# Fetching ten of 391 groups of x1 rows with one-row DMAs issued by SP and ACT, in the second layer of a graph network

## The chip, the cores and the metric

The kernel runs on one core of one Trainium2 chip. The metric is the time of one execution on the device in microseconds (us); smaller is better. The engines go by their names in the profile: PE (TensorE, matrix products; PEld is its weight load), DVE (VectorE), ACT (ScalarE), POOL (GpSimd), SP (SyncE). ACT, POOL and SP also issue DMAs. Each engine works through its own list of instructions in order, and waits on semaphores that other engines or DMAs raise.

## What is computed

Two layers of message passing over a graph of 12,500 nodes with 48 features each and 200,000 edges, sorted by their target node `dst`. Cut to what matters:

```python
# layer 0
tmp = concatenate([x[dst], x[src], edge_attr_32], axis=1)
msg = relu(tmp @ W1 + b1) @ W2 + b2
x   = layernorm(x + segment_sum(msg, dst))          # called x1 in the kernel
# layer 1
m   = relu(x[src] + edge_attr_48)
x   = layernorm(x + (1 + eps) * x + segment_sum(m, dst))
```

The change is about `x[src]` of layer 1: for every edge the row of x1 (48 floats, 192 bytes) of its source node, which can be any node.

## The kernel before

**Groups and steps.** The edges are cut into 391 groups (`NCHUNK`) of 512: 128 partitions times 4 tiles (`TPC`). Partition p of group g holds four edges, and their source numbers stand in `src_i[p, 4g : 4g+4]`, which is in SBUF for the whole kernel. Each layer is a loop over steps k (`run`): in each step several stages work, each on a group of its own, some groups ahead of or behind k. The order of instructions on every engine is this program order; no scheduler moves them. What the engines wait for is decided by semaphores, so an engine may be many steps ahead of another as long as its data and buffers allow it.

**Layer 1** has, in this order in each step k:

- `fetch1(k+5)`: POOL issues four indirect DMAs (`gather`, L201), one for each tile; each fetches 128 rows of x1 from DRAM into the tile `xs`. There are ten `xs` buffers, and a buffer comes free when the DVE addition `m` of the group that used it is done.
- `fill1(k+2)`: DVE makes the one-hot matrix `hot` (L302). Every fifth group SP loads a chunk of five groups of edge features, `e48c` (L293, 480 KB, three buffers).
- `sum1(k-1)`: PE multiplies `hot` with the messages of group k-1 (L323, tile `pa`), DVE adds the result to the running sums `agg` (L318). If the group is the last of a segment (one of 14 blocks of 896 nodes), `finish1` follows: transposes, the layer norm on DVE with two ACT instructions within (L350, L354), and an SP store of the result (L386).
- `message1(k)`: DVE adds x1 rows and edge features, `m` (L495), then ACT applies relu, `msg` (L497).
- `lead1(k)`: one piece of `products()`, and now and then an SP load of a segment of x1 (`x_seg`).

**The groups that PE fetches.** 28 groups (26, 39, 52, ...; `PE_GROUPS`) are not gathered by POOL. `products()` makes their rows on PE: DVE turns source numbers into selection matrices `o` (L525), PE multiplies them with x1, which lies in SBUF in three bf16 pieces (L530), and adds up over all 98 blocks of 128 nodes. Two groups are made at a time. One step does four blocks: 4 DVE comparisons and 32 matmuls; 364 of the steps hold such a piece. The rows made this way are read by `m` as the tile `made`.

**Where x1 comes from.** Layer 0 ends each segment with `finish0`, whose result SP writes to `x1_dram` (L368). Since a source may be any node, every fetch of layer 1 waits for all 14 writes.

**In layer 0** POOL gathers the rows of x (tile `cat`), and SP does in each step a load of one number from SBUF into a register (L409, `off`) and a DMA whose address in DRAM is that register (L412, `wcat<-a`, 48 rows of 512 bytes), beside a chunk of edge features each fifth group (`e32c`, L293).

**ACT** does one relu a step in layer 1 and next to nothing else; **SP** issues a chunk load each fifth step, and 28 loads and stores of segments.

Of the kernel before, what the change touches and what calls it, by code (L numbers as in the profile page):

```python
# [24 lines left out]
F32 = mybir.dt.float32  # L25
# [6 lines left out]
P = 128  # L32
# [3 lines left out]
D = 48  # L36
# [5 lines left out]
NPAD = NT * Q  # L42
TPC = 4
CHUNK = P * TPC
NCHUNK = -(-E // CHUNK)
# [12 lines left out]
EC = 5  # L58
# [4 lines left out]
PIECES = 3  # L63
BPS = 4

PE_GROUPS = [FIRST + EVERY * i for i in range(NPE)]
assert PE_GROUPS[-1] < NCHUNK and NPE % BATCH == 0

assert NSEG * NB == NT
# [28 lines left out]
@with_exitstack  # L98
def gnn_kernel(
    ctx: ExitStack,  # L100
    tc: tile.TileContext,
    x: bass.AP,
    src: bass.AP,
    dst: bass.AP,
    e32: bass.AP,
    e48: bass.AP,
    w1: bass.AP,
    b1: bass.AP,
    w2: bass.AP,
    b2: bass.AP,  # L110
    eps: bass.AP,
    out: bass.AP,
):
    nc = tc.nc
    flag_pool = ctx.enter_context(tc.tile_pool(name="flag", bufs=1))
    dram = ctx.enter_context(tc.tile_pool(name="dram", bufs=1, space=bass.MemoryType.DRAM))
    flag = flag_pool.tile([1, 1], I32, name="flag")
    with ExitStack() as fast:
        windowed(fast, tc, dram, flag, x, src, dst, e32, e48, w1, b1, w2, b2, eps, out)
    misfit = nc.values_load(  # L120
        flag, engines=[mybir.EngineType.PE, mybir.EngineType.DVE, mybir.EngineType.Activation,
                       mybir.EngineType.Pool, mybir.EngineType.SP],
        min_val=0, max_val=2 * P,
    )
    with tc.If(misfit > 0), ExitStack() as slow:
        general(slow, tc, dram, x, src, dst, e32, e48, w1, b1, w2, b2, eps, out)


def windowed(ctx, tc, dram, flag, x, src, dst, e32, e48, w1, b1, w2, b2, eps, out):
    nc = tc.nc  # L130
# [3 lines left out]
    echunk = ctx.enter_context(tc.tile_pool(name="echunk", bufs=3))  # L134
    work = ctx.enter_context(tc.tile_pool(name="work", bufs=2))
    aggs = ctx.enter_context(tc.tile_pool(name="aggs", bufs=3))
    node = ctx.enter_context(tc.tile_pool(name="node", bufs=2))
# [4 lines left out]
    src_i = const.tile([P, NCHUNK * TPC], I32, name="src_i")  # L142
# [6 lines left out]
    def load_seg(table, s):  # L149
        x_seg[s] = seg.tile([Q, NB, D], F32, name="x_seg")  # L150
        nc.sync.dma_start(
            x_seg[s], table[s * SN : (s + 1) * SN, :].rearrange("(t p) d -> p t d", p=Q)
        )
# [43 lines left out]
    x1_dram = dram.tile([NPAD, D], F32, name="x1_dram")  # L197
    xp = const.tile([Q, NT, PIECES, D], BF16, name="xp")

    def gather(t, table, g, j):  # L200
        nc.gpsimd.indirect_dma_start(  # L201
            out=t, out_offset=None, in_=table,
            in_offset=bass.IndirectOffsetOnAxis(
                ap=src_i[:, g * TPC + j : g * TPC + j + 1], axis=0
            ),
        )
# [41 lines left out]
    def split_src():  # L248
# [3 lines left out]
        )[:, :, 0:TPC]  # L252
        last = src_i[:, PE_GROUPS[-1] * TPC : (PE_GROUPS[-1] + 1) * TPC]
        bits = node.tile([P, NPE, TPC], I32, name="bits")
# [31 lines left out]
    chunk = {}  # L286

    def load_edges(name, table, width, g):
        c = g // EC
        if g % EC == 0:  # L290
            n = min(EC, NCHUNK - g)
            chunk[name] = echunk.tile([P, EC, TPC * width], F32, name=name)
            nc.sync.dma_start(  # L293
                chunk[name][:, :n, :],
                table[g * CHUNK : (g + n) * CHUNK, :].rearrange(
                    "(c p t) d -> p c (t d)", p=P, t=TPC
                ),
            )
        return chunk[name][:, g % EC, :].rearrange("p (t d) -> p t d", t=TPC)

    def one_hot(o, g):
        nc.vector.tensor_tensor(  # L302
# [85 lines left out]
    def last_group(s):  # L388

        return max(g for g in range(NCHUNK) if low(g) < (s + 1) * SN)  # L390
# [6 lines left out]
    cat, ph, h, pm, hot = {}, {}, {}, {}, {}  # L397
# [6 lines left out]
    def fill0(g):  # L404
        e = load_edges("e32c", e32, DE, g)
        nc.scalar.activation(cat[g][:, :, W + D :], e, AF.Copy)
        one_hot(cat[g][:, :, :W], g)
        s = seg_of(g)
        at = nc.sync.value_load(  # L409
            off[0:1, g : g + 1], min_val=low(g) - seg_start(s), max_val=high(g) - seg_start(s)  # L410
        )
        nc.sync.dma_start(wcats[g % NW][0:W, :], a_dram[s][bass.ds(at, W), :])  # L412
# [65 lines left out]
    made = {}  # L478

    def fetch1(g):  # L480
        if g in PE_GROUPS:
            return
        cat[g] = cats.tile([P, TPC, D], F32, name="xs")
        for j in range(TPC):
            gather(cat[g][:, j, :], x1_dram, g, j)

    def fill1(g):
        hot[g] = work.tile([P, TPC, W], F32, name="hot", bufs=4)
        one_hot(hot[g], g)
        h[g] = load_edges("e48c", e48, D, g)  # L490

    def message1(g):
        m = work.tile([P, TPC, D], F32, name="m")
        xs = made.pop(g) if g in PE_GROUPS else cat.pop(g)
        nc.vector.tensor_tensor(m, xs, h[g], op=ALU.add)  # L495
        msg = work.tile([P, TPC, D], F32, name="msg1")
        nc.scalar.activation(msg, m, AF.Relu)  # L497
        h[g] = msg
# [10 lines left out]
    def place(first):  # L509

        which = psum.tile([Q, tiles, P], BF16, name="pt", bufs=2)
        for i in range(BATCH):
            which_e = work.tile([P, TPC, Q], BF16, name="which_e")
            for j in range(TPC):
                nc.vector.tensor_scalar(
                    which_e[:, j, :], iota_q, part[:, first + i, j : j + 1],
                    block[:, first + i, j : j + 1], op0=ALU.is_equal, op1=ALU.mult,
                )
            for j in range(TPC):
                nc.tensor.transpose(which[:, i * TPC + j, :], which_e[:, j, :], ident16)  # L520
        return which

    def select(which, b):
        o = onehots.tile([Q, tiles, P], BF16, name="o")
        nc.vector.tensor_scalar(o, which, float(b + 1), None, op0=ALU.is_equal)  # L525
        return o

    def multiply(ps, o, b):
        for k in range(tiles):
            nc.tensor.matmul(  # L530
                ps[k // PER][:, k % PER, :], o[:, k, :], xp[:, b, :, :],
                start=False, stop=False, skip_group_check=True,
            )

    def edge_of(ps, start):
        for t in ps:
            n = t.shape[1] * PIECES * D
            nc.tensor.matmul(
                t.rearrange("p k c d -> p (k c d)"), zeros[:, :P], zeros[:, :n],
                start=start, stop=not start,  # L540
            )
# [4 lines left out]
    def products():  # L546

        for first in range(0, NPE, BATCH):
            due = PE_GROUPS[first]
            which = place(first)  # L550
            ps = [
                psum.tile([P, min(PER, tiles - k * PER), PIECES, D], F32, name=name,
                          bufs=2 if name == "pt" else 1)
                for k, name in enumerate(SUMS)
            ]
            edge_of(ps, True)
            last = []
            for b in range(0, NT, BPS):
                now = [(b + i, select(which, b + i)) for i in range(min(BPS, NT - b))]
                for c, o in last:  # L560
                    multiply(ps, o, c)
                last = now
                yield due
            for c, o in last:
                multiply(ps, o, c)
            edge_of(ps, False)
            xs = work.tile([P, tiles, D], F32, name="made")
            for k, t in enumerate(ps):
                n = t.shape[1]
                nc.vector.tensor_reduce(  # L570
                    xs[:, k * PER : k * PER + n, :], t.rearrange("p k c d -> p k d c"),
                    AX.X, ALU.add,
                )
            for i in range(BATCH):
                made[PE_GROUPS[first + i]] = xs[:, i * TPC : (i + 1) * TPC, :]
            yield due

    work1 = products()

    def lead1(k):  # L580
        next(work1, None)
        for s in range(NSEG):
            if k == last_group(s) - 6:
                load_seg(x1_dram, s)

    run([(fetch1, -AHEAD), (fill1, -2), (sum1, 1), (message1, 0)], finish1, lead1)


# [209 lines left out]
```

## Time and profile before

| | |
|---|---|
| Time, median of 11 runs | 4841.38 us (4819.24 to 4860.51) |
| The profiled execution: its time / its span | 4848.64 us / 4846.9 us |
| Layer 1 in it: first and last start of `m` | 2549.7 us, 4833.8 us |
| First 320 starts of `m` / the other 71 | 1924.10 us / 360.20 us |
| Indirect DMAs of POOL in layer 1 | 1452, of 966 ns each |
| POOL idle before them until `m` freed a buffer | 463.2 us, in 152 places |
| ACT idle before its relu, until `m` was done | 1615.2 us, in 306 places |
| Mean granted clock of TensorE | 0.726 of full speed |

The profile is of one execution on the chip. Times are in us from the first instruction unless marked ns. "Busy" counts the engine's own work; register, branch and semaphore instructions and the issuing of DMAs are not counted, but the trace has their records, under an engine's name with a q (SPq, ACTq). In a list of waits a line gives the engine and the line of the code, what ended the wait, the total idle time in us, how often, and the longest one. "issue" is idle time in which an engine waited for nothing that the profile shows; "remote" is a releaser that it can't name. A row of the timeline gives start, duration, engine, line, operation, tiles (out<-in), shape, how many were merged, and in brackets the idle time before it and what ended it.

### The profile page before, as it was taken

The page shows a single profiled execution, that of the slowest core. Times are in us where ns is not written, and L with a number is a line of the kernel's source. Part 1 is how long each engine was busy: PE and PEld are TensorE (multiplying, and loading weights), DVE is VectorE, ACT ScalarE, POOL GpSimd, SP SyncE. Part 2 cuts the span into 40 slices and gives each one's busy share as a digit, 9 for nine tenths or more (in the row PEclk, how much of TensorE's full clock was granted, in tenths as well). Part 3 has the DMA queues.
Part 4 walks back from the last instruction along what each step waited for, and adds up shares of the span by engine and source line. Part 5 has one row for each costly group of instructions (what it writes and reads, how often), then busy time and mean ns, then how long its engine had stood idle before and what let it go on. Part 6 is the DMA issues. An engine that isn't in the chain of part 4 may idle for free. (4 is left out here: it accounts for less than half of the span.)

```text
span 4846.9 us, 67581 instructions
## 1 busy us (share of the span) xinstructions
PE 3171.6 (65%) x23396; PEld 2395.9 (49%) x23396; DVE 1899.0 (39%) x4618; ACT 563.2 (12%) x1329; POOL 2887.0 (60%) x3025
## 2 busy tenths in 40 slices
PE   4676676676776667767656666666666676666652
PEld 3454454454454445545435555555555555555541
DVE  1222222222222222222225555555555555555542
ACT  1111111111111111111110000000000000000000
POOL 5655655655665566566646565656565665655564
PEclk7777767777677777677767777777777777777765
DMA  2111111111111111111111111111111111111111
GB/s 53 32 38 38 33 36 36 35 35 38 35 37 38 31 36 39 38 32 38 33 32 30 33 30 39 34 35 34 35 34 36 34 40 34 30 39 35 34 31 35
DMA packets 293005, 171.68 MB, mean 35 GB/s; under 512 B 109664, under 2 KB 292400, under 8 KB 292656
## 3 DMA queue, kind: packets, MB, share of 16 engines
q0 software_dynamic: 96512, 74.31, 10.2%
q1 hardware_dynamic: 179248, 84.31, 6.4%
q10 hardware_dynamic: 16896, 8.69, 0.6%
q8 instruction: 185, 3.03, 0.3%
q14 instruction: 164, 1.34, 0.1%
HBM read 154.45 MB, written 12.62 MB: 34 GB/s over the span
## 5 line engine op out<-in xcount | busy, mean ns | idle before, releaser
L201 POOL DMA_INDIRECT cat<-in_x_dram,src_i x1564 | 1483.1, 948 | 971.1 <-issue 857.0
L201 POOL DMA_INDIRECT xs<-x_dram,src_i x1452 | 1401.9, 966 | 960.5 <-DVE m L495 463.2
L530 PEld LDWEIGHTS <-o 128*128 128x128 bf16 x10976 | 930.1, 117 | 591.5 <-issue 553.8
L525 DVE TENSOR_SCALAR o<-pt 128x1024 bf16<-128x1024 bf16 x1372 | 849.8, 679 | 56.3 <-remote 51.6
L424 PE MATMUL ph<-cat_t,wcat 128*128 128x512 f32 x782 | 621.9, 888 | 199.7 <-DVE cat_t L419 190.3
L530 PE MATMUL ph<-xp,o 128*128 128x144 bf16 x4116 | 636.1, 267 | 169.8 <-issue 162.1
L530 PE MATMUL pm<-xp,o 128*128 128x144 bf16 x4116 | 624.5, 267 | 151.8 <-issue 151.1
L318 DVE TENSOR_TENSOR agg<-agg,pa 48x48 f32 x782 | 153.3, 196 | 1306.1 <-remote 857.6
L419 DVE COPY cat_t<-pt 128x512 f32<-128x512 f32 x391 | 269.9, 690 | 874.7 <-PE pt L417 374.9
L432 PE MATMUL pm<-w_sb,h 128*128 128x48 f32 x3128 | 553.4, 332 | 79.1 <-ACT h L426 41.8
L530 PE MATMUL pt<-xp,o 128*128 128x144 bf16 x2744 | 501.8, 267 | 130.3 <-issue 129.6
L432 PEld LDWEIGHTS pm<-w_sb,h 128*128 128x128 f32 x3128 | 499.5, 243 | 113.5 <-ACT h L426 49.0
L323 PE MATMUL pa<-hot,msg 128*48 128x48 f32 x3128 | 317.3, 247 | 330.3 <-issue 206.8
L323 PE MATMUL pa<-cat,msg 128*48 128x48 f32 x3128 | 281.7, 249 | 376.8 <-issue 209.4
L426 ACT ACTIVATE h<-ph,b_sb 128x512 f32<-128x512 f32 x391 | 268.6, 687 | 1830.3 <-PE ph L424 779.6
L323 PEld LDWEIGHTS pa<-cat,msg 128*48 128x48 f32 x3128 | 226.8, 158 | 485.2 <-issue 300.4
L323 PEld LDWEIGHTS pa<-hot,msg 128*48 128x48 f32 x3128 | 239.0, 154 | 429.0 <-issue 264.1
L417 PEld LDWEIGHTS pt<-ident,cat 128*128 128x128 f32 x1564 | 278.0, 190 | 333.3 <-issue 317.2
L497 ACT ACTIVATE msg<-m 128x192 f32<-128x192 f32 x391 | 141.8, 363 | 2077.4 <-DVE m L495 1615.2
L434 DVE TENSOR_TENSOR msg<-pm,b_sb 128x192 f32<-128x192 f32 x391 | 137.9, 353 | 544.9 <-remote 218.2
L417 PE MATMUL pt<-ident,cat 128*128 128x128 f32 x1564 | 332.1, 353 | 1.9 <-issue 1.9
L424 PEld LDWEIGHTS ph<-cat_t,wcat 128*128 128x128 f32 x782 | 160.3, 254 | 215.6 <-DVE cat_t L419 205.3
(79 smaller groups left out, 1061.6 us busy)
## 6 DMA issues: line engine op xcount, KB each, us to landing
e48c<-in_e_dram SPq DMA_DIRECT2D x78, 480.0 KB
cat<-in_x_dram,src_i POOLq DMA_INDIRECT x1564
e32c<-in_e_dram SPq DMA_DIRECT2D x78, 320.0 KB
xs<-x_dram,src_i POOLq DMA_INDIRECT x1452
wcat<-a SPq DMA_DIRECT2D x391, 24.0 KB
a<-a ACTq DMA_DIRECT2D x14, 256.0 KB
a<-a ACTq DMA_DIRECT2D x14, 192.0 KB
x_seg<-in_x_dram SPq DMA_DIRECT2D x14, 168.0 KB
```

Of the source, the lines that this page charges most:

```text
L201: nc.gpsimd.indirect_dma_start(out=t, out_offset=None, in_=table, in_offset=bass.IndirectOffsetOnAxis(ap=src_i[:, g * TPC + j : g * TPC + ...
L318: nc.vector.tensor_tensor(cols, cols, pa, op=ALU.add)
L323: nc.tensor.matmul(pa, msg[:, j, :], hot[:, j, :], start=j == 0, stop=j == TPC - 1)
L417: nc.tensor.transpose(pt[:, j, :], cat[g][:, j, :], ident[:P, :P])
L419: nc.vector.tensor_copy(cat_t, pt)
L424: nc.tensor.matmul(ph, wcats[g % NW], h[g], start=True, stop=True)
L426: nc.scalar.activation(t, ph, AF.Relu, bias=b1_sb)
L432: nc.tensor.matmul(pm[:, j, :], h[g][:, j, :], w2_sb, start=True, stop=True)
L434: nc.vector.tensor_tensor(msg, pm, b2_sb[:, None, :].to_broadcast([P, TPC, D]), op=ALU.add)
L497: nc.scalar.activation(msg, m, AF.Relu)
L525: nc.vector.tensor_scalar(o, which, float(b + 1), None, op0=ALU.is_equal)
L530: nc.tensor.matmul(ps[k // PER][:, k % PER, :], o[:, k, :], xp[:, b, :, :], start=False, stop=False, skip_group_check=True,)
```

## The change

Ten groups are taken from POOL and fetched row by row: five by SP (67, 132, 197, 262, 327) and five by ACT (74, 139, 204, 269, 334). For each partition the engine loads that partition's four source numbers from `src_i` into registers (one load instruction), then issues four DMAs, each of one row of 192 bytes, whose address in `x1_dram` comes from a register. Each engine does two partitions, so eight DMAs, in each step; a group takes 64 steps and a 65th without a fetch. The first begins in step -5, the last ends in step 318. The rows are read by `m` as the tiles `rows_sync` and `rows_scalar`, two buffers each. Besides, `load_edges`, which both layers use, now issues the load of a chunk of edge features when the chunk before it is first used, five groups sooner; the first two chunks are loaded together.

```diff
+BY_ROW = {"sync": (67, 65, 2), "scalar": (74, 65, 2)}
+ROW_GROUPS = {
+    name: list(range(first, NCHUNK, every)) for name, (first, every, _) in BY_ROW.items()
+}
+ALL_ROW_GROUPS = sum(ROW_GROUPS.values(), [])
...
     def load_edges(name, table, width, g):
         c = g // EC
-        if g % EC == 0:
-            n = min(EC, NCHUNK - g)
-            chunk[name] = echunk.tile([P, EC, TPC * width], F32, name=name)
+        for k in ((0, 1) if g == 0 else (c + 1,) if g % EC == 0 else ()):
+            first = k * EC
+            n = min(EC, NCHUNK - first)
+            if n <= 0:
+                continue
+            chunk[name, k] = echunk.tile([P, EC, TPC * width], F32, name=name)
             nc.sync.dma_start(
...
     def fetch1(g):
-        if g in PE_GROUPS:
+        if g in PE_GROUPS + ALL_ROW_GROUPS:
             return
...
     def message1(g):
-        xs = made.pop(g) if g in PE_GROUPS else cat.pop(g)
+        xs = made.pop(g) if g in made else cat.pop(g)
...
-    work1 = products()
+    rows_by = {
+        name: ctx.enter_context(tc.tile_pool(name=f"rows_{name}", bufs=2)) for name in BY_ROW
+    }
+
+    def fetch_rows(name):
+        engine = getattr(nc, name)
+        kind = {"sync": mybir.EngineType.SP, "scalar": mybir.EngineType.Activation}[name]
+        for g in ROW_GROUPS[name]:
+            t = rows_by[name].tile([P, TPC, D], F32, name=f"rows_{name}")
+            per_step = BY_ROW[name][2]
+            for p in range(P):
+                _, at = nc.values_load_multi_w_load_instructions(
+                    src_i[p : p + 1, g * TPC : (g + 1) * TPC], engines=[kind],
+                    min_val=0, max_val=NPAD - 1,
+                    skip_runtime_bounds_check_because="src holds node numbers",
+                )
+                for j in range(TPC):
+                    engine.dma_start(t[p : p + 1, j, :], x1_dram[bass.ds(at[j], 1), :])
+                if p % per_step == per_step - 1:
+                    yield
+            made[g] = t
+            yield
+
+    work1 = [products()] + [fetch_rows(name) for name in BY_ROW]
 
     def lead1(k):
-        next(work1, None)
+        for w in work1:
+            next(w, None)
```

In the compiled lists PE and DVE keep their instructions in number and order; POOL has 40 indirect DMAs fewer; SP and ACT each have 640 register loads and 2560 DMAs more, each with an address computation before it. Every one of these DMAs waits for one of eight semaphores that all DMAs of SP and ACT share, that is, for an earlier DMA that used the same one to land. For stretches of some steps SP uses four of them and ACT four others; where a chunk load comes between, they change places.

More of the change, by code (lines that the diff above doesn't have):

```diff
@@ L64 @@
 BPS = 4
+BY_ROW = {"sync": (67, 65, 2), "scalar": (74, 65, 2)}
[3 more added lines that the diff above has]
+ALL_ROW_GROUPS = sum(ROW_GROUPS.values(), [])
 PE_GROUPS = [FIRST + EVERY * i for i in range(NPE)]
+assert len(set(ALL_ROW_GROUPS + PE_GROUPS)) == len(ALL_ROW_GROUPS + PE_GROUPS)
 assert PE_GROUPS[-1] < NCHUNK and NPE % BATCH == 0
@@ L289, in load_edges @@
         c = g // EC
-        if g % EC == 0:
-            n = min(EC, NCHUNK - g)
-            chunk[name] = echunk.tile([P, EC, TPC * width], F32, name=name)
+        for k in ((0, 1) if g == 0 else (c + 1,) if g % EC == 0 else ()):
[4 more added lines that the diff above has]
+            chunk[name, k] = echunk.tile([P, EC, TPC * width], F32, name=name)
             nc.sync.dma_start(
-                chunk[name][:, :n, :],
-                table[g * CHUNK : (g + n) * CHUNK, :].rearrange(
+                chunk[name, k][:, :n, :],
+                table[first * CHUNK : (first + n) * CHUNK, :].rearrange(
                     "(c p t) d -> p c (t d)", p=P, t=TPC
@@ L298, in load_edges @@
             )
-        return chunk[name][:, g % EC, :].rearrange("p (t d) -> p t d", t=TPC)
+        return chunk[name, c][:, g % EC, :].rearrange("p (t d) -> p t d", t=TPC)
     def one_hot(o, g):
```

## The prediction

> **What bounds the kernel now.** I read the waits first, then one line's view, then the timeline. All ten groups taken from POOL are in layer 1, so the question is whether layer 1 waits for POOL. The list of waits of POOL, then the view of line L495, where DVE reads the gathered rows:
>
> ```profile
> POOL xs L201 <- DVE m L495: 463.2, 152, 10.6
> POOL xs L201 <- issue: 437.9, 1264, 33.1
> ```
>
> ```profile
> L495 DVE TENSOR_TENSOR m<-xs,e48c x363: 340/357/433, 2549.7 to 4833.8; 128x192 f32<-128x192 f32 x182
> ...
> its engine sat idle before it (us, times) until:
>   issue: 2.3, 6
> ```
>
> POOL waits for `m`: it is ten buffers ahead and stands still 463 us of the layer. In the other direction there is nothing: DVE idled 2.3 us in all before 391 `m`, and never for a gather. A group costs POOL four gathers at a pitch of 1.25 us (0.95 busy, 0.30 idle, in the POOL timeline), 5.0 us, and 363 of 391 groups are gathered, so 363 x 5.0 = 1820 us of the layer's 2284. POOL is not the bound.
>
> What is? The timeline of DVE (the `m` alone, one a step) and of PE in the longest of these steps:
>
> ```profile
> 3006.74 0.36 DVE L495 TENSOR_TENSOR m<-xs,e48c 128x192 f32<-128x192 f32 x1
> ...
> 3009.80 0.34 DVE L495 TENSOR_TENSOR m<-xs,e48c 128x192 f32<-128x192 f32 x1
> ...
> 3017.59 0.36 DVE L495 TENSOR_TENSOR m<-xs,e48c 128x192 f32<-128x192 f32 x1
> ...
> 3024.85 0.34 DVE L495 TENSOR_TENSOR m<-made,e48c 128x192 f32<-128x192 f32 x1
> ```
>
> ```profile
> 3018.79 0.24 PE L323 MATMUL pa<-hot,msg 128*48 128x48 f32 x1 [0.81 <-issue]
> 3019.49 0.24 PE L323 MATMUL pa<-hot,msg 128*48 128x48 f32 x1 [0.47 <-issue]
> 3020.21 0.30 PE L323 MATMUL pa<-hot,msg 128*48 128x48 f32 x1 [0.48 <-issue]
> ```
>
> Steps take 3.1 us, then 7.8 and 7.3. In the long ones PE gets its instructions one or two at a time, 0.7 us apart, and waits for no engine. PE's own instruction supply sets the pace, DVE waits for its sums and POOL for DVE. The first 320 steps, those beside the new fetches, take 1924.10 us: **6.01 us a step**.
>
> **Removed.** 40 gathers, 40 x 1.25 = 50 us of POOL. POOL then waits some 510 us instead of 463. Worth nothing on the path. What would be late next for these groups are the rows that SP and ACT fetch.
>
> **Added on SP.** The nearest rows are layer 0's register load and register-addressed DMA, in the views of L409 and L412:
>
> ```profile
> L409 SPq TENSOR_LOAD <-off x391: 5/268/711, 13.4 to 2465.1; - x196
> ...
> L412 SPq FUSED_REGOPS  x391: 3/42/1420, 14.2 to 2465.6; - x196
> L412 SPq MOVE wcat<-a x391: 2/13/712, 14.4 to 2465.8; - x196
> L412 SPq DMA_DIRECT2D wcat<-a x391: 14/316/1395, 23.2 to 2467.1; - x196
> ```
>
> Medians are in the middle, in ns. With the usual 0.03 to 0.06 us between records: a row is 0.042 + 0.056 (address) + 0.013 + 0.026 (move) + 0.316 + 0.045 (DMA) = 0.50 us. A partition is one load, 0.268 + 0.046 = 0.31, and four rows, 1.99: 2.31. Two partitions a step: **4.6 us**. The DMA's price is that of 48 rows of 512 bytes; one row could be cheaper, and issued straight behind another DMA it could be dearer (ACT's second store in a row took 0.52 after 0.38 at 1516). That bounds a step between 4.0 and 6.2.
>
> SP has instruction stalls too: among its 3080 records 247 have 0.6 to 0.8 us of nothing before them, all but a few at places where it waits for no one (the maxima of 0.7 and more above). That is 0.70 x 247 / 3080 = 0.056 us an instruction; 26 instructions a step make 1.5 us. The lower end is 0, as on ACT, whose 3012 records have no such gap; the upper end is PE's bad stretches, four instructions each 0.7 us, 4.5 us. I take SP's own rate, since it is SP.
>
> Each fifth step adds a chunk load: 0.37 + 0.05 us of issue. The rows reuse four semaphores, so the fourth DMA behind the load waits until the load has landed, 3.4 us after its issue in the trace (median of 79), less the 1.9 us gone by: together 1.9 / 5 = 0.4 us a step. Between rows alone the reuse costs nothing: a `wcat` landed 1.4 us after its issue, and four rows take 2.0 to issue.
>
> SP: 4.6 + 1.5 + 0.4 = 6.5 us, times 64/65 for the step without a fetch: **6.4 us a step**, against the 6.01 that layer 1 has.
>
> **Added on ACT.** The same rows and its relu, 0.36 + 0.1: 5.1 us without stalls, 6.6 with SP's. ACT is now idle 1615 us waiting for `m`, which is the cover. Queued behind the rows are the next relu, for which PE's sum waits, and the two ACT instructions in each layer norm, for which DVE waits. The register loads are weighed here against a rule. The Trainium skill, in "DMA: Bandwidth & Descriptors", section "Latency and other measured facts", gives a `tensor_load` a floor of some 600 ns; this trace has 268 ns on SP. By the page SP's step would be 0.7 us longer, which would make the sum below some 200 us larger; the trace decides.
>
> **Do the two add up or overlap?** A SP 0.4 us slower than the step would use up its slack of eight steps (a group's last row is issued in step 58 for `m` in step 67) by group 132. The shared semaphores take even that: whenever the sets change places, SP's row waits for an ACT row of the same step and the other way, so the slower sets the pace of both, and ACT's relu carries it to PE.
>
> To see what a pace A does to uneven steps I replayed the 320 measured ones: relu k starts no sooner than `m` and than A after relu k-1, and PE starts step k+1 when its own measured work of step k and relu k are done. The loss: A = 5.1: 16 us; 6.0: 46; 6.2: 86; 6.4: 140; 6.5: 170; 7.5: 473. Below 6 the one step between relu and sum absorbs nearly all; above it each tenth costs 32 us.
>
> **Moved: edge loads.** In layer 0 a chunk load now needs a buffer that ACT emptied six groups earlier, while SP's own `wcat` waits for PE's work of four groups earlier: no new wait. In the trace ACT waited 1.6 us in all for this line: no gain. In layer 1 the first load stands behind 24 rows, some 15 us after x1 is written at 2487, and ACT's first relu behind five steps of rows, at about 2520; the first `m` is at 2549.7 since PE needs that long for its first products. Hidden; if PE were faster there, 10 us.
>
> **Sum.** Fewer gathers: 0; edge loads: 0; pace 6.4: +140 us; layer norms behind rows: eleven of them, from 0 to 5 us each, of which I take 0, as the replay holds the steps' own lengths. The profiled execution had 4848.6 us, so 4988.6; the median of the runs lies 7 below it: **4982 us, +2.9%**.
>
> **Rivals.**
> - *The fetches fit under the steps* (no stalls in SP's dense list, A = 5.1 to 5.9). For it: ACT and DVE show no such gaps, and SP's may come from standing idle. Against: SP's are there. +16 to +40 us: 4860 to 4880, slower by 0.4 to 0.8%; with A at 5 or less, or if PE uses the waits to fill its instruction supply, within 0.3%.
> - *Issue is much dearer* (0.65 us a row, or stalls as on PE, or the semaphores lock SP and ACT to each other). A = 7.5: 5310 us. At 9.1, PE's bad rate throughout, +980; I leave that out.
> - *Faster.* One mechanism: PE's stalls shrink when POOL issues 40 gathers fewer, or when ACT spaces the steps out. It takes 15 us, 2% of the 670 us that PE so loses in the first 320 steps (35% of them lie in gaps of 0.45 to 1.3 us between its instructions), and A under 5. For it: the stalls are the bound. Against: such gaps fill 35% of the time in which POOL gathers and 34% of that in which it stands still. At best the 50 us that POOL no longer spends: 4800.
> - *The change doesn't do what it says*: no; the lists show the rows on SP and ACT.
>
> **How the numbers follow.** Within 0.3% (14.5 us) counts as the same, about what a measurement can tell from no change. Pace above the steps (A 6.0 to 7.0; 4890 to 5160): 0.50. Fits under: 0.27, of which 0.13 within 0.3%. Much dearer: 0.15, up to 5310 for most of it. Faster: 0.08. Slower 0.79, same 0.13, faster 0.08. Eight in ten lie between 4840 and 5250.
>
> A rule speaks against the change as a whole: "Rules for kernel authors" on the same page of the skill wants many small transfers coalesced, since they pay mostly overhead. Here a row's 192 bytes cost 0.5 us of an engine, 512 rows 256 us, where POOL's gathers take 5.0 us.
>
> **What would show it.** Right: SP and ACT have a register-addressed DMA each 0.5 to 0.6 us and hardly any idle time in the first 320 steps; `m` comes at an even 6.2 to 6.6 us instead of 3 and 8; PE waits for ACT `msg` far more than 121.7 us; POOL waits for `m` longer than 463 us; the last 71 steps stay at 360 us. Wrong: 3 us steps still there (rows cheaper or no stalls), or a row at 0.7 us or more.

## The result and the profile after

| | before | after |
|---|---|---|
| Time, median (lowest to highest) | 4843.15 us (4819.24 to 4861.45; 31 runs) | 5081.56 us (5073.45 to 5101.26; 8 runs) |
| Ratio, 95% interval | | 1.0502 (1.0483 to 1.0521) |
| First 320 starts of `m` | 1924.1 us, 6.01 a step | 2162.9 us, 6.76 a step |
| The other 71 | 360.2 us | 354.0 us |
| First start of `m` | 2549.7 us | 2546.1 us |

The change costs 238 us, and the first 320 steps, those beside the fetches, are 239 us longer. Layer 0 and the rest of layer 1 give and take 10 us at most. Lines behind the change move by 9 to 13 (`m` is now L508, relu L510, POOL's gathers L210, the sum L336, the products L543); L603 is the load of the source numbers, L609 the DMA of a row. The windows of line L508 in the kernel after, with the columns window, length, DVE busy in these instructions and their number, granted clock, DMA share, GB/s:

```profile
2546.10:4709.00 2162.90, 113.84 (x320) 0.72 0.16 31
4709.00:5063.00 354.00, 24.95 (x71) 0.66 0.17 35
```

The waits of the kernel after, all engines:

```profile
ACT msg L510 <- DMA rows_scalar<-x_dram: 1108.0, 160, 70.1
...
POOL xs L210 <- DVE m L508: 808.6, 245, 13.5
...
PEld pa L336 <- ACT msg L510: 568.6, 189, 12.0
PE pa L336 <- ACT msg L510: 523.0, 178, 11.8
...
PEld L543 <- issue: 203.3, 233, 2.7
```

A new first line: ACT's relu stands behind ACT's own row DMAs. PE's sum waits 523 us for that relu, where the kernel before had this line:

```profile
PE pa L323 <- ACT msg L497: 121.7, 79, 11.7
```

POOL waits 809 us for `m` instead of 463. The supply of PE's instructions is no longer what is late in most steps: in the first 320 the gaps of 0.45 to 1.3 us from the start of one PE instruction to the start of the next shrank from 673 to 166 us in all, while the longer gaps grew from 166 to 846 us. The timeline of ACT in the kernel after shows one such step (ACTq is the issuing of the DMAs; the last bracket is the idle time before the relu):

```profile
3001.51 0.36 ACT L510 ACTIVATE msg<-m 128x192 f32<-128x192 f32 x1 [5.31 <-DMA rows_scalar<-x_dram]
3002.23 6.80 ACTq L609 DMA_DIRECT2D rows_scalar<-x_dram  x8
3009.41 0.36 ACT L510 ACTIVATE msg<-m 128x192 f32<-128x192 f32 x1 [7.53 <-DMA rows_scalar<-x_dram]
```

Eight rows take ACT 6.8 us between two relus. And DVE, whose `m` came 3.1, 7.8 and 7.3 us apart before:

```profile
3056.48 0.34 DVE L508 TENSOR_TENSOR m<-rows_scalar,e48c 128x192 f32<-128x192 f32 x1
3064.32 0.36 DVE L508 TENSOR_TENSOR m<-xs,e48c 128x192 f32<-128x192 f32 x1
3071.12 0.36 DVE L508 TENSOR_TENSOR m<-xs,e48c 128x192 f32<-128x192 f32 x1
3075.06 0.36 DVE L508 TENSOR_TENSOR m<-xs,e48c 128x192 f32<-128x192 f32 x1
```

Steps of 7.8, 6.8 and 3.9 us; the median of the 320 is 6.73. What makes a row step last that long is in the views of lines L603 and L609 (duration in ns: least, median, most):

```profile
L603 SPq TENSOR_LOAD <-src_i x640: 3/557/769, 2480.6 to 4709.5; - x160
L603 ACTq TENSOR_LOAD <-src_i x640: 3/583/1257, 2482.3 to 4704.8; - x160
```

```profile
L609 SPq FUSED_REGOPS  x2560: 2/37/1402, 2481.0 to 4711.7; - x197
L609 SPq MOVE rows_sync<-x_dram x2560: 2/29/1459, 2481.1 to 4711.8; - x197
L609 SPq DMA_DIRECT2D rows_sync<-x_dram x2560: 2/228/785, 2482.5 to 4711.8; - x197
...
L609 ACTq DMA_DIRECT2D rows_scalar<-x_dram x2560: 3/235/1396, 2483.0 to 4707.1; - x197
```

I added up SP's records between 2600 and 4400 us. SP never rests: it fetches 525 partitions in 1799 us, 6.85 us for the two of a row step, and since one step in 65 has none, 6.75 us a step. At their median durations and spacings these records, chunk loads and stores included, take 1205 us (4.59 a row step). The other 593 us are some 66 of waiting for chunk loads to land, 35 of waiting for semaphores last used by ACT's rows (together 0.38 a row step), and 492 us without a releaser (1.9 a row step), nearly all of it, 460 us, in 829 pieces of 0.4 to 0.8 us. ACT's own list would take some 5.2 us a step by its medians, and 6.5 with its stalls and waits where it is alone (*act_only* below); here it also waits some 160 to 240 us, by how the stalls within are counted, for semaphores that SP's rows used last. So I read that **SP paces ACT, and ACT's relu paces PE**; no run gives the two engines semaphores of their own. The list of SP's own waits agrees that SP hardly waits for anyone:

```profile
SPq L609 <- DMA rows_sync<-x_dram: 46.0, 88, 1.4
...
SPq L609 <- DMA e48c<-in_e_dram: 35.9, 26, 2.4
...
SPq L609 <- DMA rows_scalar<-x_dram: 1.2, 2, 0.7
```

(The list puts some waits down to the row DMA before them; the sums above go by the semaphore that each row waits for.)

### The profile page after: what moved, and what is told of

It reads as the page before. It is cut to its first block, busy times and chain, and to the rows that moved or that the text cites. A ratio compares the mean times of both kernels' runs of the same rounds, so it can differ in the third digit from the quotient of the medians.

```text
span 5075.6 us, 84190 instructions
## 1 busy us (share of the span) xinstructions
PE 3183.0 (63%) x23396; PEld 2487.2 (49%) x23396; DVE 1909.7 (38%) x4618; ACT 563.1 (11%) x1329; POOL 2830.6 (56%) x2985
## 5 line engine op out<-in xcount | busy, mean ns | idle before, releaser
L210 POOL DMA_INDIRECT xs<-x_dram,src_i x1412 | 1345.3, 953 | 1255.7 <-DVE m L508 808.6
L210 POOL DMA_INDIRECT cat<-in_x_dram,src_i x1564 | 1483.4, 948 | 961.0 <-issue 849.9
L543 PEld LDWEIGHTS <-o 128*128 128x128 bf16 x10976 | 1010.3, 125 | 230.6 <-issue 203.3
L336 PE MATMUL pa<-hot,msg 128*48 128x48 f32 x3128 | 296.1, 254 | 904.8 <-ACT msg L510 523.0
L336 PEld LDWEIGHTS pa<-hot,msg 128*48 128x48 f32 x3128 | 235.7, 162 | 999.5 <-ACT msg L510 568.6
L543 PE MATMUL pm<-xp,o 128*128 128x144 bf16 x4116 | 649.4, 280 | 62.7 <-issue 62.5
L543 PE MATMUL ph<-xp,o 128*128 128x144 bf16 x4116 | 652.0, 281 | 58.3 <-issue 57.2
L445 PE MATMUL pm<-w_sb,h 128*128 128x48 f32 x3128 | 564.1, 336 | 69.5 <-ACT h L439 47.0
L445 PEld LDWEIGHTS pm<-w_sb,h 128*128 128x128 f32 x3128 | 509.9, 247 | 103.5 <-ACT h L439 54.4
L543 PE MATMUL pt<-xp,o 128*128 128x144 bf16 x2744 | 514.4, 278 | 45.7 <-issue 45.5
L336 PE MATMUL pa<-cat,msg 128*48 128x48 f32 x3128 | 283.8, 250 | 392.5 <-issue 196.5
L336 PEld LDWEIGHTS pa<-cat,msg 128*48 128x48 f32 x3128 | 228.6, 159 | 501.7 <-issue 283.7
L510 ACT ACTIVATE msg<-m 128x192 f32<-128x192 f32 x391 | 141.8, 363 | 2341.6 <-DMA rows_scalar<-x_dram 1108.0
```

The lines of the kernel that those rows point to most:

```text
L210: nc.gpsimd.indirect_dma_start(out=t, out_offset=None, in_=table, in_offset=bass.IndirectOffsetOnAxis(ap=src_i[:, g * TPC + j : g * TPC + ...
L336: nc.tensor.matmul(pa, msg[:, j, :], hot[:, j, :], start=j == 0, stop=j == TPC - 1)
L445: nc.tensor.matmul(pm[:, j, :], h[g][:, j, :], w2_sb, start=True, stop=True)
L543: nc.tensor.matmul(ps[k // PER][:, k % PER, :], o[:, k, :], xp[:, b, :, :], start=False, stop=False, skip_group_check=True,)
```

## The experiments

**A** is the prediction's theory: the list of SP, in part that of ACT, sets a pace, and a step lasts as long as the longer of this pace and its own work. Below the length of a step a row then costs nothing. The rival **C**: each row costs its share wherever it is issued, full list or not. A further idea, that the two lists lose time by holding each other up, is told apart by the runs that have only one of them. A third question is what the 40 gathers were worth.

The runs fell on several chips, and each is compared with the kernel before on its own chip. One of these chips was of another kind, as shown under *edges_only*.

| run | its time, us | before there, us | ratio, 95% | first 320 steps, us |
|---|---|---|---|---|
| sp_only | 5032.3 | 4913.4 | 1.0233 (1.0201 to 1.0266) | 2062.6 |
| act_only | 5016.3 | 4913.4 | 1.0189 (1.0147 to 1.023) | 2045.1 |
| static_rows | 4977.3 | 4913.4 | 1.0131 (1.0103 to 1.0159) | 2010.7 |
| thin | 4944.7 | 4913.4 | 1.0064 (1.0044 to 1.0085) | 1984.3 |
| edges_only | 3851.7 | 3851.1 | 0.9999 (0.999 to 1.0009) | 1509.9 |
| no_fetch | 3806.3 | 3851.1 | 0.9877 (0.9861 to 0.9894) | 1474.6 |
| half_pe | 3920.5 | 3851.1 | 1.0175 (1.0158 to 1.0192) | 1570.0 |
| half_pe_again | 4859.2 | 4839.3 | 1.0037 (1.0011 to 1.0063) | 1970.4 |
| dense | 5645.5 | 4839.3 | 1.1623 (1.1564 to 1.1681) | 2710 |
| after_again | 5097.7 | 4839.3 | 1.052 (1.0468 to 1.0572) | 2168.1 |
| no_fetch_again | 4790.0 | 4845.5 | 0.9887 (0.9858 to 0.9916) | 1878.3 |
| after_third | 5100.6 | 4845.5 | 1.0531 (1.0496 to 1.0565) | 2173 |

### One list at a time: sp_only and act_only

Half of the groups go back to POOL, so that only SP (*sp_only*, the first diff) or only ACT (*act_only*, the second) fetches rows.

```diff
-BY_ROW = {"sync": (67, 65, 2), "scalar": (74, 65, 2)}
+BY_ROW = {"sync": (67, 65, 2)}
```

```diff
-BY_ROW = {"sync": (67, 65, 2), "scalar": (74, 65, 2)}
+BY_ROW = {"scalar": (74, 65, 2)}
```

> SP's five groups by row stay, ACT's five go back to POOL. Theory A (the pace of SP's own list, 4.6 us of issue and some 2 us of instruction stalls a step, sets the step): nearly all of the loss stays, since SP falls behind, `m` waits for its rows and chunk loads queue behind them; only the eight steps of slack (some 50 us) may be saved: 5010 to 5080 us. Theory B (ACT's rows hold back the relu behind them): 4840 to 4870. Theory C (each added instruction or DMA costs the same, through the instruction supply or the DMA rings, whoever issues it): half the loss, 4960.

> ACT's five groups by row stay, SP's five go back to POOL. A: ACT's own pace is 5.0 us a step with its relu and 0.6 of stalls, below the 6.0 of the step before: 4860 to 4890 us, and ACT no longer waits for rows of SP. B: nearly all of the loss stays, 5040 or more. C: 4960.

With SP alone, SP's list is as full as in the kernel after: 540 partitions in 1799 us, 6.66 us a row step, of which 564 us are beyond the medians. So SP's list needs no rows on ACT to be that long; the two lists holding each other up is not where it comes from. The relu now follows `m` at once (0.09 us), and the one DVE wait that names SP's list is for chunk loads that come late, in the view of `m` of *sp_only*:

```profile
  DMA e48c<-in_e_dram: 47.1, 18
```

That is 47 us of the loss; the rest has no releaser's name (idle time of PE before its sum without one, 416 us in the kernel before, is 560 here). This last rise is no mark of a full list: *static_rows* below, whose lists are short, has 538. Nor did SP use up its slack, as the prediction had it: `m` waits 0.8 us in all for SP's rows; the steps took 2062.6 us, only 36 less than 320 steps of SP's list (2099), and less than eight steps of slack. The time, at 1.0233, is near half of the change's loss, as C says (4960 of 4841 is 1.025), and below A's range (5010 to 5080 of 4841 are 1.035 to 1.049): the 5032 us lie in that range only because the kernel before is slower on this chip too. Only SP's full list speaks for A here, and how it costs the steps 2% without a late relu is not shown.

With ACT alone, A's pace of 5.6 us was too low (it expected a ratio of 1.004 to 1.010). ACT's list took 6.50 us a row step (277 of them in 1800 us): 5.2 by its medians, where the first DMA behind a load takes 0.47 us and the others 0.235, 0.8 of stalls, which ACT's records before had none of, and about 0.5 of waiting for transfers to land. The waits of *act_only*:

```profile
ACT msg L510 <- DMA rows_scalar<-x_dram: 799.5, 138, 10.8
...
PE pa L336 <- ACT msg L510: 366.1, 190, 13.2
```

ACT's list reaches PE without SP's help, then: 320 steps at 6.50 x 64/65 = 6.40 us are 2048 us, and the first 320 steps took 2045.1. Either list alone is longer than a step of 6.0 us.

### Shorter rows and fewer rows: static_rows and thin

*static_rows* (the first diff) issues as many DMAs with fixed addresses and without the register loads, so it fetches other rows than the reference's. *thin* (the second) takes four groups instead of ten, one partition a step.

```diff
-                _, at = nc.values_load_multi_w_load_instructions(
...
-                    engine.dma_start(t[p : p + 1, j, :], x1_dram[bass.ds(at[j], 1), :])
+                    engine.dma_start(t[p : p + 1, j, :], x1_dram[p * TPC + j : p * TPC + j + 1, :])
```

```diff
-BY_ROW = {"sync": (67, 65, 2), "scalar": (74, 65, 2)}
+BY_ROW = {"sync": (132, 130, 1), "scalar": (139, 130, 1)}
```

> All 5120 one-row DMAs stay, but with fixed addresses (always the first 512 rows of x1), so that the register loads, address computations and moves are gone: the result of the ten groups is another one, and a step has 8 instructions of SP instead of 26. A: SP's pace falls to some 2.3 to 3 us a step, and the time to 4840 to 4860 us. If the DMAs themselves (their landing, the shared semaphores, the rings) set the pace: over 5000. C by instructions: 4915, C by DMAs: 5080.

> One partition a step instead of two on both engines: two groups each (132, 262 and 139, 269) in 128 steps, so four of ten groups are left and the pace of either list is halved. A, with its threshold at the step's 6.0 us: SP needs 3.4 us a step, no loss: 4840 to 4860 us. C: four tenths of the loss, 4935.

Most of the loss goes when the lists become short, which A says; but 1.3% and 0.6% stay, where A had at most 0.4%. *thin* is also well below the 2% of C. The relu of *static_rows* follows `m` by 0.09 us in the median and is later than that by 16 us in all 320 steps together, so nearly all that is left does not come through the relu. If the kernel without any fetch would be some 50 us better here too (measured below, on another chip, for 40 gathers; 20 us for 16), the rest is 114 us for 5120 rows and 51 us for 2048: 22 and 25 ns a row. Such a **small cost for each row below the pace** is in neither theory as A was put; what it is stays open. PE's gaps above 1.3 us are 307 us in *static_rows* and 272 in *thin*, against 166, but that 166 is from a profile of before on another chip.

### Edge loads alone: edges_only

```diff
-BY_ROW = {"sync": (67, 65, 2), "scalar": (74, 65, 2)}
+BY_ROW = {}
```

> The second part of the change alone: chunk loads one chunk ahead, no row fetches. The prediction had them at nothing: 4830 to 4857 us. If the earlier loads collide with something in either layer: over 4860.

The earlier loads are worth nothing on this chip: 0.9999. But the run, and the two that shared its chip, showed a second kind of chip. The kernel before takes 3851 us there, not 4843, at a granted clock of 0.787 instead of 0.726; gaps of 0.45 to 1.3 us in PE's list add up to 57 us in the first 320 steps instead of 673, and SP has no pieces of 0.7 us. The waits of *edges_only*, where no rows are fetched by SP or ACT:

```profile
DVE m L508 <- DMA xs<-x_dram,src_i: 553.2, 277, 4.1
```

Here DVE waits for the gathers in most steps (277 of 391), and POOL waits 3 us for DVE: POOL is the bound, at 4.72 us a step. On this kind of chip the change itself was never run.

### What the gathers were worth: no_fetch and no_fetch_again

The additions of the ten groups read a tile of zeros, and nobody fetches their rows. The second run is the same kernel on a chip of the usual kind.

```diff
-    work1 = [products()] + [fetch_rows(name) for name in BY_ROW]
+    spare = const.tile([P, TPC, D], F32, name="spare")
+    nc.vector.memset(spare, 0.0)
+    for g in ALL_ROW_GROUPS:
+        made[g] = spare
+    work1 = [products()]
```

> The ten groups are fetched by nobody: their `m` reads a tile of zeros, so the result of these groups is another one. It keeps what the change gains (40 gathers fewer on POOL) and the earlier chunk loads, without the rows. A: POOL is not the bound, no gain, 4830 to 4857 us, and POOL waits some 50 us longer for `m`. Rival (POOL sets the pace in places, the change gains 50 us and loses 290): 4793.

> Ten groups fetched by nobody, again (their `m` reads zeros), since the first time it fell on a chip without instruction stalls, where POOL was the bound and 40 gathers fewer gave 45 us. With stalls: POOL waits for `m` 463 us, so nothing is gained, 0.997 to 1.003 times the kernel before, and POOL's waits for `m` grow by some 50 us. If the gain were there as well, hidden in the changed kernel by a larger loss: 0.99 times.

On the chip where POOL is the bound, 45 us are gained: 40 gathers at 4.72 / 4 = 1.18 us are 47. On the usual chip POOL waits for `m` in plenty, and the prediction put the gathers at nothing. They are worth **55 us** there too. (The kernel has the earlier edge loads as well; in the kernel before ACT waits 1.6 us for such loads and `m` not at all, so I put the 55 us down to the gathers.) The waits of *no_fetch_again*, and its window of line L508:

```profile
POOL xs L210 <- DVE m L508: 465.6, 154, 10.6
```

```profile
2550.30:4428.60 1878.30, 112.93 (x320) 0.74 0.16 35
```

POOL still waits 466 us (463 before), and does not wait longer by what it was spared: the steps became shorter (1878 us, where the profile of before has 1924) by about the 50 us that POOL no longer issues. PE's gaps of 0.45 to 1.3 us went from 673 to 633 us. Against this kernel, on the same chip, the 5120 rows cost 5100.6 - 4790.0 = 311 us; the change is 311 less 55.

### Is PE's number of instructions the bound? half_pe and half_pe_again

In the kernel before, PE makes 12 groups instead of 28, one piece every second step, and POOL gathers the other 16.

```diff
-FIRST = 26
-EVERY = 13
-NPE = 28
+FIRST = 52
+EVERY = 26
+NPE = 12
...
-        next(work1, None)
+        if k % 2 == 0:
+            next(work1, None)
```

> The kernel before, with 12 groups made by PE instead of 28, one piece of the products each second step; POOL gathers the other 379. If PE with its instruction supply is the bound of layer 1 and POOL has 463 us of slack, this is faster although POOL gets 64 gathers more: POOL's own time is 379 x 5.0 = 1900 us and half of the pieces are gone, so 4500 to 4650 us. If POOL is the bound, slower by 64 x 1.25 = 80 us: 4920.

> The kernel before with 12 groups made by PE instead of 28, again. Where PE has no instruction stalls it was 1.0175 times the kernel before, since POOL was the bound. Where it has them, theory A (PE's instruction supply is the bound, POOL has 463 us of slack) gives 0.93 to 0.96 times; if POOL were the bound there too, 1.0175 as well.

On the chip where POOL is the bound, *half_pe* is 69 us slower; 64 gathers more at 1.18 us are 76. On the usual chip it is 1.0037 times the kernel before, neither the 0.93 to 0.96 nor the 1.0175 that were expected: PE had 14.7 thousand instructions in the first 320 steps instead of 25 thousand, and yet they took 1970 us. The timeline of DVE in *half_pe_again*:

```profile
3028.84 0.36 DVE L495 TENSOR_TENSOR m<-xs,e48c 128x192 f32<-128x192 f32 x1
3038.95 0.36 DVE L495 TENSOR_TENSOR m<-xs,e48c 128x192 f32<-128x192 f32 x1
3040.94 0.36 DVE L495 TENSOR_TENSOR m<-xs,e48c 128x192 f32<-128x192 f32 x1
```

A step of 10.1 us and one of 2.0. PE within the long one and behind it:

```profile
3032.87 0.24 PE L323 MATMUL pa<-hot,msg 128*48 128x48 f32 x1 [1.82 <-issue]
3034.27 0.31 PE L323 MATMUL pa<-hot,msg 128*48 128x48 f32 x1 [1.16 <-issue]
3036.36 0.24 PE L323 MATMUL pa<-hot,msg 128*48 128x48 f32 x1 [1.79 <-issue]
...
3039.82 0.88 PE L323 MATMUL pa<-hot,msg 128*48 128x48 f32 x8 [1.12 <-ACT msg L497]
```

The sum's own few instructions come one at a time in the long step, and eight within 0.9 us in the next. That PE's instruction supply sets the steps by the number of PE's instructions is refuted; that it sets them is not. On the other chip the time for each gather that POOL issues in the first 320 steps is 1.27 to 1.28 us in all three kernels. On the usual kind it is 1924 / 1188 = 1.62 us (before), 1878 / 1156 = 1.62 (*no_fetch_again*) and 1970 / 1270 = 1.55 (*half_pe_again*). The steps thus behave somewhat as though POOL's list bounded them, though POOL is seen waiting; but a fixed time a step (6.01, 5.87 and 6.16 us) fits these three about as well. Whether and how the gathers lengthen PE's stalls is not settled; no run tested it.

### Twice the rows in half the steps: dense

```diff
-BY_ROW = {"sync": (67, 65, 2), "scalar": (74, 65, 2)}
+BY_ROW = {"sync": (67, 65, 4), "scalar": (74, 65, 4)}
...
-        name: ctx.enter_context(tc.tile_pool(name=f"rows_{name}", bufs=2)) for name in BY_ROW
+        name: ctx.enter_context(tc.tile_pool(name=f"rows_{name}", bufs=5)) for name in BY_ROW
```

> The same ten groups, rows and instructions, with four partitions a step instead of two, so that they all lie in the first 160 steps (five row buffers an engine instead of two, else the same). Theory A: what counts is a list's time in a step against the step: an engine needs 3.3 to 3.4 us a partition with stalls (2.3 to 2.6 without), 13.5 us a step for 160 steps, where the step has 6.0 (4.7): some 1200 us more than the kernel before with stalls, 800 to 900 without. Theory C (a price for each row, wherever it stands): as the changed kernel, 1.05 times the kernel before.

The number of rows is the same, so C gives the same loss as the change's; measured is +806 us, where the change on the same chip (*after_again*) costs 258. The windows of line L508 in *dense* (the rows end about step 160, inside the second window), and its wait of PE:

```profile
2573.70:4000.00 1426.30, 45.98 (x129) 0.62 0.09 20
4000.00:5284.00 1284.00, 67.53 (x191) 0.70 0.14 32
```

```profile
PE pa L336 <- ACT msg L510: 1136.1, 204, 28.8
```

11.06 us a step beside the rows. SP fetched 617 partitions in 1774 us, 2.87 us each and so 11.5 for four; one step in 33 has none, which makes 11.15 a step: **the steps follow SP's list**, and C falls. A's own size was too high (some +1200): with SP's list twice as dense, a partition cost 2.27 by its medians and 0.60 of stalls and waits, where the change has 2.30 and 1.13.

### The change again: after_again and after_third

> The changed kernel again, beside the runs below on one chip. The kernel before took 4841 us where the change was measured, 4913 in the first set of runs, 3851 in the second, where PE shows next to no instruction stalls (57 us in the first 320 steps instead of 673). If this set falls on a place with stalls: 1.04 to 1.05 times the kernel before, as measured. If on one without: steps there take 4.7 us, POOL sets their pace, and SP and ACT without stalls need 4.6 and 5.2 us: theory A gives a gain of 45 us on POOL and a loss of (5.2 - 4.7) x 320 = 160, so 1.02 to 1.04 times the kernel before.

> The changed kernel beside it. With stalls 1.05 times the kernel before, as twice before, and SP's list filling the first 320 steps without a rest (6.7 to 6.8 us a step). On a chip without stalls, which it has not yet met: SP's list needs 4.6 us, ACT's 5.2 with its relu, the step has 4.7: 45 us won on POOL, up to 160 lost on ACT, 1.00 to 1.04.

1.052 and 1.0531 on two chips, with the first 320 steps at 2173 us in the second; SP's list in it is as full as in the first profile (1200 us by the medians and 599 beyond in 1799). The finding does not hang on one chip of the usual kind.

## Why the prediction was right, and where not

- **Added on SP**: 6.85 us a row step, where the prediction had 6.5. Its 4.6 of issue measured 4.59, but that was luck, by two errors that nearly cancel: a row took 0.41 us, not 0.50 (the DMA 0.228, not 0.316), and the load 0.61, not 0.31; it reads four numbers where the row of the profile before (268 ns) reads one, though no run tests that this is why. These make 4.5, and the issue of chunk loads and stores the rest. The Trainium skill's floor of some 600 ns in "DMA: Bandwidth & Descriptors", "Latency and other measured facts", was nearer (medians of 557 and 583 ns in this profile, just under it). The prediction's 0.4 for chunk loads and semaphores measured 0.38, but it was made up otherwise: 0.25 of waiting for chunk loads and 0.13 for ACT's rows, which the prediction had not put in.
- **The term that was mis-sized is SP's stalls**: 1.9 us a row step instead of 1.5 (0.072 us an instruction instead of 0.056). The direction and the range held, and the size did not. With 6.75 us a step the replay of the steps before gives +244 us instead of +140; measured are +239. The 104 us between the two replays account for the 99 by which the forecast of 4982 fell short.
- **Added on ACT**: 5.1 to 6.6 us; 5.2 by the medians, and 6.50 in full where it is alone, the upper end. That ACT has no stalls was true of the sparse list of before only.
- **Do the two add up or overlap?** Right, as far as the trace shows: ACT waits some 160 to 240 us for semaphores of SP's rows and SP some 35 us for ACT's, so the slower list paces both, and ACT's relu, late by 3.5 us in the median where it had been late by 0.09, carries it to PE. What the prediction didn't see is that either list alone suffices for some 2%, SP's even without a late relu.
- **Removed: worth nothing**: this step failed. Without the fetches the 40 gathers less give 55 us. It did not show in the change's time, since that is a maximum and not a sum: 320 steps of SP's list at 6.75 are 2160 us, of 2162.9 measured, however short the steps could otherwise be. Replayed by the prediction's rule at 6.75 us, the 320 steps of *no_fetch_again* end within 2 us of those of the kernel before.
- **The rival "faster"** had the mechanism (fewer gathers, shorter steps) and a fair price, at best 50 us. The argument against it, that PE's gaps are as frequent when POOL stands still as when it gathers, was no evidence: *no_fetch_again* has the gain with the same waits of POOL.
- **"PE's own instruction supply sets the pace"**: seen in the timeline, but not by PE's number of instructions (*half_pe_again*).
- **Moved edge loads**: nothing, as predicted (0.9999), measured alone on the other kind of chip only.
- **What would show it**: `m` came at 6.76 us, above the 6.2 to 6.6; PE's wait for `msg` 523 us and POOL's for `m` 809, both up as said; the last 71 steps 354 us, as said. "Hardly any idle time" holds for SP. "Even" does not: steps of 3 to 4 us are still among those of 6.7 and 8 (41 of the 320 are under 4, where 126 were before).

Open: the 22 to 25 ns a row that *static_rows* and *thin* lose without a late relu; what *sp_only* loses without a late relu; whether and how gathers lengthen PE's stalls; and what the change does on a chip without the stalls. Rows with semaphores that SP and ACT don't share were not tried. No kernel here that fetches all rows beats the one before.

## What to carry to other kernels

Small DMAs on an engine that looks idle are priced by what they make of that engine's list in one step, stalls included, set against the length of the step: under it they cost less (here some 22 to 25 ns a row), above it the list is the step, and whatever was saved elsewhere is lost in the maximum. An engine that the trace shows waiting may still be worth relieving; leave its work out once and measure. And take the load and the DMA that one prices by in the shape that the change will use: four numbers and one row are not one number and 48 rows.

## What was not expected of the hardware

- The same kernel takes 3851 us on one chip and 4839 to 4913 us on the others, and what the traces show of the difference is gaps of 0.45 to 1.3 us from one PE instruction to the next (57 us in 320 steps of *edges_only* against 673 in the kernel before), idle pieces of 0.6 to 0.8 us on SP (none against 247) and the clock (0.787 against 0.726). Why the chips differ is not shown. What bounds the kernel is another engine on the one than on the others.
- The stalls went with the chip and with the list, and not with the engine alone: ACT, with none among its 3012 records before but where it waited, had 0.8 us a row step once its list was dense (*act_only*), and SP's came down from 1.13 us a partition, waits included, to 0.60 when its list was twice as dense.
- A register-addressed DMA of one row took 0.228 us to issue on SP and 0.235 on ACT, but 0.47 on ACT straight behind a register load.
